# Attention's output set on feature rows through memory, divided there, and projected without transposes

## The chip, the cores and the metric

The kernel runs on one core of a Trainium2 chip. A core has five engines that run side by side, each through its own list of instructions in order: TensorE (PE in the profile; PEld is its weight load), VectorE (DVE), ScalarE (ACT), GpSimd (POOL) and SyncE (SP). SP does no arithmetic here; it issues nearly all transfers between HBM and the core's memory, in the order of its list, and a transfer that has to wait for something holds up all transfers behind it on SP. Matmul results land in PSUM, everything else lies in SBUF, both with 128 partitions.

The metric is the device time of one execution in microseconds (us). Lower is better.

## The reference

One sequence of 2048 rows with 256 features, all in float32. The program is

```python
x = x + attn_a(layernorm(x))   # 16 heads of 16, 4 key/value heads, rope, biases, causal
x = x + ffn(layernorm(x))      # 256 -> 2048 -> 256, 4-bit weights with scales, gelu gate
x = x + attn_b(layernorm(x))   # 16 heads of 16, no rope, causal
x = x + ffn(layernorm(x))      # the same weights again
```

and both attentions end in

```python
probs = jax.nn.softmax(scores, axis=-1)
attended = jnp.einsum('bhts,bshd->bthd', probs, v).reshape(B, S, hidden)
return attended @ Wo.T + bo
```

(the second has no bias). The change concerns what lies between the product with v and the product with Wo.

## The kernel before, in words

**Tiling.** The rows are cut into NB = 4 blocks of TB = 512, each of NT = 4 tiles of 128. The 16 heads are cut into NG = 4 groups of four. Attention works through 16 units (block b, group g), block by block. Because of the causal mask block b looks at 4(b + 1) key tiles, so a unit is short in block 0 (12 to 16 us where nothing else is done in it) and 41 to 54 us in block 3.

**A unit.** `value_steps(b, g)` gives the main list. `pair(kt, p)` makes the scores of two heads with key tile kt, keys on partitions and queries along the row (L716), subtracts the row maximum by a further matmul (L721), and lets ScalarE take the exponential (L729). `values(half)` multiplies the exponentials by v (L703), four heads at once, each into its own 32 partitions of one PSUM tile `ps_av`. Of the 32 partitions of a head the first 16 are its attended features, the 17th is the sum of the exponentials (v carries a column of ones), the others are padding. At the end of a unit `end()` copies this tile to SBUF as `o` (ScalarE, L739): features on partitions, queries along the row.

**Beside it** runs a side list. `weave` puts its steps between the main ones, in proportion. It has, above all, `max_steps` of the unit that follows: scores again, queries on partitions (L643), whose row maxima VectorE takes (L651), and a `gather` of them. Scores of both kinds use three PSUM buffers in turn (`ps_s`); a fourth, single tile (`ps_m`) serves everything else. In units g = 0 and 1 the side list also prepares the next block (`prep_steps`: layernorm, transposes, projections, bias and rope; the results go to HBM as a high and a low part and come back in another layout), and in the first attention a share of the dequantization of the MLP's weights. `load_q` for the unit after next stands at the head of each unit: eight transfers on SP, 64 KB each (L614).

**After a unit**, as the first step of the next one's side list, `divide()` transposes `o` in four pieces of 128x128 (L746), so that queries are on partitions; VectorE takes the reciprocals of the sums (L751) and multiplies (L754), into `self.att[b]`. When all four groups of a block are there, `out_steps` (in the next block's first unit) transposes att back in pieces, features on partitions (`turn`, L775), copies them as `aT` (ScalarE, L780), multiplies by Wo (`project`, L787) and adds to x (VectorE, L792). So each attended value is transposed twice: once to be divided, once to be projected.

**At the end of attention** the last `divide`, two empty steps and the last `out_steps` are handed to the MLP, as side steps among the features of its first block. A feature step is eight matmul records on TensorE (L876), then ScalarE, GpSimd and VectorE for the gelu gate. The side list there also prepares the MLP's second block. `Mlp.run` begins with the load of the down weights `wd`, 2 MB, on SP (L868).

Every engine runs its list in the order written[...].

Of the kernel before, what the change touches and what calls it, by code (L numbers as in the profile page):

```python
# [8 lines left out]
F32 = mybir.dt.float32  # L9
# [7 lines left out]
ALU = mybir.AluOpType  # L17
# [3 lines left out]
P = 128  # L21
S = 2048
D = 256
NH = 16
HD = 16
NKV = 4
NG = NH // 4
MLP = 2048
NFC = MLP // P
TB = 512  # L30
NB = S // TB
NT = TB // P
# [23 lines left out]
def blend(a, b):  # L56

    keyed = [((n + 0.5) / len(a), 0, n, f) for n, f in enumerate(a)]
    keyed += [((n + 0.5) / len(b), 1, n, f) for n, f in enumerate(b)]
    return [f for *_, f in sorted(keyed, key=lambda k: k[:3])]  # L60
# [3 lines left out]
def tile_hybrid_layers(  # L64
# [25 lines left out]
    nc = tc.nc  # L90
# [9 lines left out]
    small = ctx.enter_context(tc.tile_pool(name="small", bufs=2))  # L100
    pre = ctx.enter_context(tc.tile_pool(name="pre", bufs=1))
    psum = ctx.enter_context(tc.tile_pool(name="psum", bufs=1, space=PSUM))
    dram = ctx.enter_context(tc.tile_pool(name="dram", bufs=1, space=bass.MemoryType.DRAM))
# [7 lines left out]
    def ps_m():  # L111
        return psum.tile([P, 512], F32, tag="m", name="ps_m")
# [36 lines left out]
    for src, at in ((bq, 0), (bk, D), (bv, D + 64)):  # L149
        n = src.shape[1]  # L150
# [18 lines left out]
    ident = const.tile([P, P], F32, tag="ident", name="ident")  # L169
# [221 lines left out]
    class Attention:  # L391
# [293 lines left out]
        def value_steps(self, b, g):  # L685

            nk = NT * (b + 1)
            held = {"pending": []}

            def values(half):  # L690

                kt, q0, es_ = held["pending"][0]
                few = TB - q0 <= TB // 2
                if half == 1:
                    held["pending"].pop(0)
                    if few:
                        return
                elif kt == 0:
                    held["av"] = ps_av()
                own = slice(q0, TB) if few else slice(*((q0, TB // 2), (TB // 2, TB))[half])  # L700
                for j in range(4):
                    h = g if self.first else 4 * g + j
                    nc.tensor.matmul(  # L703
                        held["av"][32 * j : 32 * j + 32, own],
                        lhsT=self.vv[kt // NT][:, kt % NT, h * VW : h * VW + 32],
                        rhs=es_[j // 2][:, j % 2, own],
                        start=(kt == 0 and half == 0), stop=(kt == nk - 1),
                    )

            def pair(kt, p):  # L710
                q0 = max(0, kt - NT * b) * P
                diagonal = kt >= NT * b
                keys = slice((kt % NT) * P, (kt % NT + 1) * P)
                pt = ps_s()
                for r in range(2):
                    nc.tensor.matmul(  # L716
                        pt[:, r, q0:], lhsT=self.key_rows(kt // NT, g, p, r, keys),
                        rhs=self.qT[b, g][64 * r : 64 * r + 64, p, q0:], start=True, stop=False,
                    )
                for r in range(2):  # L720
                    nc.tensor.matmul(  # L721
                        pt[:, r, q0:], lhsT=sel[64 * r : 64 * r + 64, p, :],
                        rhs=self.mT[b, g][64 * r : 64 * r + 64, q0:],
                        start=False, stop=not diagonal,
                    )
                if diagonal:
                    self.add_mask(pt, 1, q0)
                e = self.wk.tile([P, 2, TB], F32, tag="e", name="e", bufs=4)
                nc.scalar.activation(e[:, :, q0:], pt[:, :, q0:], AF.Exp, scale=QK_SCALE)  # L729
                if p == 0:  # L730
                    held["es"] = [e]
                else:
                    held["pending"].append((kt, q0, held["es"] + [e]))

            def end():
                values(0)
                values(1)
                o = pre.tile([P, TB], F32, tag="o", name="o")
                nc.scalar.copy(o, held["av"])  # L739
                held["o"] = o  # L740

            def divide():
                o = held["o"]
                pt = ps_m()
                for i in range(NT):
                    nc.tensor.transpose(  # L746
                        pt[:, i * P : (i + 1) * P], o[:, i * P : (i + 1) * P], ident
                    )
                heads = pt.rearrange("p (t j c) -> p t j c", t=NT, c=32)
                rec = small.tile([P, NT, 4], F32, tag="rec", name="rec")  # L750
                nc.vector.reciprocal(rec, heads[:, :, :, HD])  # L751
                if g == 0:
                    self.att[b] = pre.tile([P, NT, NG, 4, HD], F32, tag="att", name="att")
                nc.vector.tensor_tensor(  # L754
                    self.att[b][:, :, g], heads[:, :, :, :HD],
                    rec.unsqueeze(3).broadcast_to([P, NT, 4, HD]), ALU.mult,
                )

            steps = []
            for kt in range(nk):  # L760
                for p in range(2):
                    steps.append(lambda kt=kt, p=p: pair(kt, p))
                    if kt:
                        steps.append(lambda p=p: values(p))
            return steps, end, divide

        def out_steps(self, b):
            held = {}

            def turn(n):  # L770
                pt = ps_m()
                for i in range(2):
                    flat = self.att[b][:, 2 * n + i].rearrange("p g j c -> p (g j c)")
                    for c in range(2):
                        nc.tensor.transpose(  # L775
                            pt[:, (2 * i + c) * P : (2 * i + c + 1) * P],
                            flat[:, c * P : (c + 1) * P], ident,
                        )
                aT = pre.tile([P, 2, 2, P], F32, tag="aT", name="aT")
                nc.scalar.copy(aT, pt.rearrange("p (i c t) -> p i c t", i=2, c=2))  # L780
                held[n] = aT

            def project(n):
                po = ps_m()
                for i in range(2):
                    for c in range(2):
                        nc.tensor.matmul(  # L787
                            po[:, i * D : (i + 1) * D], lhsT=held[n][:, i, c, :],
                            rhs=self.wo[:, c, :], start=(c == 0), stop=(c == 1),
                        )  # L790
                to = xt[b][:, 2 * n : 2 * n + 2, :]
                nc.vector.tensor_tensor(  # L792
                    to, po.rearrange("p (i d) -> p i d", i=2), to, ALU.add
                )

            return [lambda n=n, f=f: f(n) for n in range(2) for f in (turn, project)]

        def run(self, extra, beside):


            units = [(b, g) for b in range(NB) for g in range(NG)]
            per_unit = -(-len(extra) // (len(units) - NG))
            late, ahead = [], []
            for n, (b, g) in enumerate(units):
                more = []
                if g == 0 and b > 0:
                    more += self.out_steps(b - 1)
                if g == 0 and b + 1 < NB:
                    ahead = self.prep_steps(b + 1)
                    few = -(-len(ahead) // 2)  # L810
                if n >= NG:
                    more, extra = more + extra[:per_unit], extra[per_unit:]
                if g < 2:
                    more, ahead = more + ahead[:few], ahead[few:]
                if n + 2 < len(units):
                    self.load_q(*units[n + 2])
                steps, turn = [], None
                if n + 1 < len(units):
                    steps, turn = self.max_steps(*units[n + 1])
                else:  # L820
                    more += beside
                side = late + (blend(steps, more) if steps else more)
                steps, end, divide = self.value_steps(b, g)
                weave(steps, side, rest=4)
                if turn:
                    turn()
                end()
                late = [divide]
            return late + [lambda: None] * 2 + self.out_steps(NB - 1)


    class Mlp:
# [89 lines left out]
    at = Attention(True, wqkv_a)  # L922
    with tc.tile_pool(name="wk1", bufs=2) as wk, tc.tile_pool(name="kv1", bufs=1) as kv:
        at.wk = at.qpool = wk
        with tc.tile_pool(name="init", bufs=1) as pool:
# [13 lines left out]
            steps, turn = at.max_steps(0, 0)  # L939
# [5 lines left out]
    at = Attention(False, wqkv_b)  # L945
    with tc.tile_pool(name="kv20", bufs=1, reuse_waits="tile") as kv0, tc.tile_pool(
        name="wk2", bufs=2, reuse_waits="tile"
# [7 lines left out]
        steps, turn = at.max_steps(0, 0)  # L955
# [60 lines left out]
```

## Time and profile before

| | us |
|---|---|
| median of 3 runs (1912.67 to 1927.99) | 1915.32 |
| the profiled execution | 1916.85 |
| its span, first to last instruction | 1914.7 |
| TensorE busy | 1829.9 |
| VectorE busy | 1109.2 |
| ScalarE busy | 813.5 |
| GpSimd busy | 238.0 |

The profile is of one execution, so sums made from it are set against its own 1916.85 us. Attention of the first layer ends at 646.5 us, the first MLP runs to about 1007, the second attention ends at 1567.9, and the second MLP closes the span. "PE ... <- ACT aT L780" in a list of waits reads: TensorE stood still until ScalarE had written aT at line 780. The duration of a matmul includes the length of the pipeline; how much of TensorE one takes is the distance from its start to the start of the next. All engines but TensorE have idle time, which costs nothing in itself.

### The profile page before, as it was taken

The numbers are of one execution on the slowest core, as the hardware profiler recorded it, in microseconds if no ns is written. First come the engines' busy times: TensorE is split into PE (matmuls) and PEld (weight loads), VectorE is DVE, ScalarE is ACT, GpSimd is POOL, SyncE is SP. The second block draws the span as 40 slices with busy tenths as digits, with TensorE's granted clock in tenths as the row PEclk, the third lists the DMA queues.
The fourth block names the chain that finished last, engine by engine and source line by source line (L and its number), as shares of the span: only waits on it lengthen the run. The fifth ranks groups of instructions, "written<-read, shape, count | busy, mean of one in ns | idle before, by whom it ended". The sixth has DMA issues, their size and how long they took to land. (4 is left out here: it accounts for less than half of the span.)

```text
span 1914.7 us, 31770 instructions
## 1 busy us (share of the span) xinstructions
PE 1829.9 (96%) x13452; PEld 985.9 (51%) x13452; DVE 1109.2 (58%) x1612; ACT 813.5 (42%) x1069; POOL 238.0 (12%) x433
## 2 busy tenths in 40 slices
PE   5899989999999999999999999999999999999999
PEld 3454444444444456656565545445444444756656
DVE  4556677787776253444444667766867715363443
ACT  1334445465666521222214355556556662131221
POOL 3301311300001011112102010010000001011110
PEclk8879999999999999999999899999999999999999
DMA  4510320301101100002305050050000010000000
GB/s 102 131 45 23 72 46 23 73 23 23 34 23 34 45 6 0 1 0 47 75 1 111 24 100 23 13 100 23 13 13 1 2 46 0 11 1 11 6 6 11
DMA packets 42270, 64.23 MB, mean 34 GB/s; under 512 B 13840, under 2 KB 20880, under 8 KB 41872
## 3 DMA queue, kind: packets, MB, share of 16 engines
q1 hardware_dynamic: 33488, 45.93, 8.5%
q0 software_dynamic: 7680, 15.74, 5.1%
q8 instruction: 106, 1.74, 0.4%
q10 hardware_dynamic: 960, 0.52, 0.1%
q14 instruction: 36, 0.29, 0.1%
HBM read 44.24 MB, written 17.83 MB: 32 GB/s over the span
## 5 line engine op out<-in xcount | busy, mean ns | idle before, releaser
L729 ACT ACTIVATE e<-ps_s 128x1024 f32<-128x1024 f32 (+3 forms) x640 | 571.5, 897 | 457.8 <-PE ps_s L628 227.8
L651 DVE TENSOR_REDUCE mx<-ps_s 128x2 f32<-128x1024 f32 (+3 forms) x640 | 657.9, 1061 | 171.0 <-PE ps_s L643 85.9
L703 PE MATMUL ps_av<-e,v 128*32 128x256 f32 (+1 forms) x4608 | 363.9, 383 | 0.7 <-ACT e L729 0.7
L643 PE MATMUL ps_s<-kT,qT 64*128 64x512 f32 (+3 forms) x1280 | 281.8, 436 | 31.3 <-DVE mx L651 12.2
L716 PE MATMUL ps_s<-qT,kT 64*128 64x512 f32 (+3 forms) x1280 | 289.9, 449 | 11.4 <-DVE mx L651 6.1
L876 PE MATMUL ps_s<-xnT,wg 128*128 128x512 f32 x512 | 242.5, 596 | 0.0
L721 PE MATMUL ps_s<-mT,sel 64*128 64x512 f32 (+3 forms) x1280 | 240.9, 372 | 0.2 <-ACT mT L677 0.2
L876 PE MATMUL ps_s<-xnT,wu 128*128 128x512 f32 x512 | 240.6, 592 | 0.0
L643 PEld LDWEIGHTS ps_s<-kT,qT 64*128 64x128 f32 x1280 | 124.3, 187 | 186.1 <-issue 85.4
L716 PEld LDWEIGHTS ps_s<-qT,kT 64*128 64x128 f32 x1280 | 122.3, 187 | 158.6 <-issue 80.9
L884 DVE TENSOR_TENSOR t<-ps_s,t 128x512 f32<-128x512 f32 x128 | 88.2, 689 | 171.2 <-POOL t L883 169.4
L882 ACT ACTIVATE t<-ps_s 128x512 f32<-128x512 f32 x128 | 76.3, 596 | 249.9 <-PE ps_s L876 249.5
L885 ACT ACTIVATE t<-t 128x512 f32<-128x512 f32 x128 | 80.6, 630 | 201.2 <-DVE t L884 201.2
L703 PEld LDWEIGHTS ps_av<-e,v 128*32 128x32 f32 x4608 | 92.7, 108 | 136.6 <-issue 113.4
L876 PEld LDWEIGHTS ps_s<-xnT,wu 128*128 128x128 f32 x512 | 97.3, 190 | 122.5 <-issue 122.5
L883 POOL TENSOR_SCALAR t<-t 128x512 f32<-128x512 f32 x128 | 79.4, 620 | 577.7 <-ACT t L882 574.9
L876 PEld LDWEIGHTS ps_s<-xnT,wg 128*128 128x128 f32 x512 | 96.2, 192 | 106.4 <-issue 104.5
L886 DVE SCALAR_TENSOR_TENSOR t<-t,ps_s 128x512 f32<-128x512 f32 x128 | 88.1, 688 | 89.0 <-ACT t L885 89.0
L721 PEld LDWEIGHTS ps_s<-mT,sel 64*128 64x128 f32 x1280 | 124.5, 190 | 10.0 <-ACT mT L677 6.5
L628 PE MATMUL ps_s<-mask_t,mask_w 64*128 64x64 bf16 x2048 | 125.1, 199 | 0.0
L901 PE MATMUL ps_av<-wd,inter 128*128 128x256 f32 x512 | 114.5, 380 | 0.0
L901 PE MATMUL ps_m<-wd,inter 128*128 128x256 f32 x512 | 114.3, 380 | 0.0
(123 smaller groups left out, 1188.3 us busy)
## 6 DMA issues: line engine op xcount, KB each, us to landing
qT<-h SPq DMA_DIRECT2D x256, 64.0 KB, 2.3
kT<-h POOLq DMA_DIRECT2D x96, 128.0 KB, 6.1
h<-high SPq DMA_DIRECT2D x24, 256.0 KB, 3.0
h<-low SPq DMA_DIRECT2D x24, 256.0 KB, 3.3
wd<-wd_kept SPq DMA_DIRECT2D x2, 2048.0 KB, 7.8
wd_kept<-dq_d SPq DMA_DIRECT2D x4, 512.0 KB, 2.7
out<-x SPq DMA_DIRECT2D x16, 128.0 KB, 1.7
x<-x SPq DMA_DIRECT2D x3, 512.0 KB, 5.1
```

Of the source, the lines that this page charges most:

```text
L628: nc.tensor.matmul(pt[:, r, to], lhsT=mask_w[rows, kind, part, :], rhs=mask_t[rows, kind, part, :], start=False, stop=(part == 1),)
L643: nc.tensor.matmul(pt[:, r, :w], lhsT=self.qT[b, g][64 * r : 64 * r + 64, p, i * P : (i + 1) * P], rhs=self.key_rows(c, g, p, r, slice(0, w)),
L651: nc.vector.tensor_reduce(held["mx"][:, i, 2 * p : 2 * p + 2, c], pt[:, :, :w], AX.X, ALU.max)
L703: nc.tensor.matmul(held["av"][32 * j : 32 * j + 32, own], lhsT=self.vv[kt // NT][:, kt % NT, h * VW : h * VW + 32], rhs=es_[j // 2][:, j % ...
L716: nc.tensor.matmul(pt[:, r, q0:], lhsT=self.key_rows(kt // NT, g, p, r, keys), rhs=self.qT[b, g][64 * r : 64 * r + 64, p, q0:], start=True ...
L721: nc.tensor.matmul(pt[:, r, q0:], lhsT=sel[64 * r : 64 * r + 64, p, :], rhs=self.mT[b, g][64 * r : 64 * r + 64, q0:], start=False, stop=no ...
L729: nc.scalar.activation(e[:, :, q0:], pt[:, :, q0:], AF.Exp, scale=QK_SCALE)
L876: nc.tensor.matmul(pt[:, k, :], lhsT=w[:, c, fc * P : (fc + 1) * P], rhs=self.xnT[b][:, c, :], start=(c == 0), stop=(c == 1),)
L884: nc.vector.tensor_tensor(t, gate, t, ALU.mult)
L885: nc.scalar.activation(t, t, AF.Tanh, scale=GELU_C)
L886: nc.vector.scalar_tensor_tensor(t, t, 1.0, gate, ALU.add, ALU.mult)
L901: nc.tensor.matmul(po[:, :D], lhsT=inter[:, fc, i * P : (i + 1) * P], rhs=wd[:, fc, :], start=(fc == 0), stop=(fc == NFC - 1),)
```

## The change

`end()` no longer keeps `o` for a transpose. It writes it to HBM (`o_kept`, 256 KB) and at once reads two things back, all three transfers on SP: the 64 feature rows of the four heads, as dense rows, into one half of a tile `att` of 128 partitions, and the four rows of sums into `den`, cut into pieces of 32 so that they lie on 64 partitions. Two groups fill `att` and `den`; so `att[b, 0]` and `att[b, 1]` hold a block's 256 features on partitions, as the projection reads them.

After every odd group two steps go to the next unit: `invert` takes the reciprocals of `den` (VectorE), writes them to HBM and reads them back as `factor`, each head's row of 512 repeated on its 16 partitions (two transfers on SP, the second after the first has landed); `divide` multiplies att by it (VectorE). `turn` and `aT` are gone; `project` reads att as it is.

The places change too. `late` (invert, divide and, after a block's last group, the two projections) is put into the next unit's side list at positions 5, 12, 14 and 16, or at its end if it is shorter, in place of divide at its head and out_steps spread through it. At the end of attention the four steps go to the MLP without the two empty steps.

```diff
                 values(1)
                 o = pre.tile([P, TB], F32, tag="o", name="o")
                 nc.scalar.copy(o, held["av"])
-                held["o"] = o
+
+
+                kept = dram.tile([4, 32, TB], F32, tag="o", name="o_kept", bufs=2)
+                nc.sync.dma_start(out=kept.rearrange("j c t -> (j c) t"), in_=o)
+                if g % 2 == 0:
+                    self.att[b, g // 2] = (
+                        pre.tile([P, TB], F32, tag="att", name="att", bufs=2),
+                        small.tile([P, 32], F32, tag="den", name="den"),
+                    )
+                att, den = self.att[b, g // 2]
+                rows = slice(64 * (g % 2), 64 * (g % 2) + 64)
+                nc.sync.dma_start(
+                    out=den[rows], in_=kept[:, HD].rearrange("j (s q) -> j s q", q=32)
+                )
+                nc.sync.dma_start(out=att[rows], in_=kept[:, :HD])
+
+            def invert():
+                den = self.att[b, g // 2][1]
+                rec = small.tile([P, 32], F32, tag="rec", name="rec")
+                nc.vector.reciprocal(rec, den)
+
+                kept = dram.tile([8, TB], F32, tag="rec", name="rec_kept", bufs=2)
+                nc.sync.dma_start(
+                    out=kept.rearrange("h (s q) -> (h s) q", q=32), in_=rec
+                )
+                factor = pre.tile([P, TB], F32, tag="factor", name="factor")
+                nc.sync.dma_start(
+                    out=factor, in_=kept.unsqueeze(1).broadcast_to([8, HD, TB])
+                )
+                held["factor"] = factor
 
             def divide():
-                o = held["o"]
-                pt = ps_m()
-                for i in range(NT):
-                    nc.tensor.transpose(
-                        pt[:, i * P : (i + 1) * P], o[:, i * P : (i + 1) * P], ident
-                    )
-                heads = pt.rearrange("p (t j c) -> p t j c", t=NT, c=32)
-                rec = small.tile([P, NT, 4], F32, tag="rec", name="rec")
-                nc.vector.reciprocal(rec, heads[:, :, :, HD])
-                if g == 0:
-                    self.att[b] = pre.tile([P, NT, NG, 4, HD], F32, tag="att", name="att")
-                nc.vector.tensor_tensor(
-                    self.att[b][:, :, g], heads[:, :, :, :HD],
-                    rec.unsqueeze(3).broadcast_to([P, NT, 4, HD]), ALU.mult,
-                )
+                att = self.att[b, g // 2][0]
+                nc.vector.tensor_tensor(att, att, held["factor"], ALU.mult)
 
             steps = []
             for kt in range(nk):
...
                     steps.append(lambda kt=kt, p=p: pair(kt, p))
                     if kt:
                         steps.append(lambda p=p: values(p))
-            return steps, end, divide
+            return steps, end, [invert, divide] if g % 2 else []
 
         def out_steps(self, b):
-            held = {}
-
-            def turn(n):
-                pt = ps_m()
-                for i in range(2):
-                    flat = self.att[b][:, 2 * n + i].rearrange("p g j c -> p (g j c)")
-                    for c in range(2):
-                        nc.tensor.transpose(
-                            pt[:, (2 * i + c) * P : (2 * i + c + 1) * P],
-                            flat[:, c * P : (c + 1) * P], ident,
-                        )
-                aT = pre.tile([P, 2, 2, P], F32, tag="aT", name="aT")
-                nc.scalar.copy(aT, pt.rearrange("p (i c t) -> p i c t", i=2, c=2))
-                held[n] = aT
-
             def project(n):
                 po = ps_m()
                 for i in range(2):
+                    t = (2 * n + i) * P
                     for c in range(2):
                         nc.tensor.matmul(
-                            po[:, i * D : (i + 1) * D], lhsT=held[n][:, i, c, :],
+                            po[:, i * D : (i + 1) * D], lhsT=self.att[b, c][0][:, t : t + P],
                             rhs=self.wo[:, c, :], start=(c == 0), stop=(c == 1),
                         )
                 to = xt[b][:, 2 * n : 2 * n + 2, :]
...
                     to, po.rearrange("p (i d) -> p i d", i=2), to, ALU.add
                 )
 
-            return [lambda n=n, f=f: f(n) for n in range(2) for f in (turn, project)]
+            return [lambda n=n: project(n) for n in range(2)]
 
         def run(self, extra, beside):
 
...
             late, ahead = [], []
             for n, (b, g) in enumerate(units):
                 more = []
-                if g == 0 and b > 0:
-                    more += self.out_steps(b - 1)
                 if g == 0 and b + 1 < NB:
                     ahead = self.prep_steps(b + 1)
                     few = -(-len(ahead) // 2)
...
                     steps, turn = self.max_steps(*units[n + 1])
                 else:
                     more += beside
-                side = late + (blend(steps, more) if steps else more)
-                steps, end, divide = self.value_steps(b, g)
+                side = blend(steps, more) if steps else more
+
+                for at, step in zip((5, 12, 14, 16), late):
+                    side.insert(at, step)
+                steps, end, late = self.value_steps(b, g)
                 weave(steps, side, rest=4)
                 if turn:
                     turn()
                 end()
-                late = [divide]
-            return late + [lambda: None] * 2 + self.out_steps(NB - 1)
+                if g == NG - 1:
+                    late += self.out_steps(b)
+            return late
 
 
     class Mlp:
```

## The prediction

> **What bounds the kernel now.** First the page's head and busy times: which engine is full.
>
> ```profile
> span 1914.7 us, 31770 instructions
> PE 1829.9 (96%) x13452; PEld 985.9 (51%) x13452; DVE 1109.2 (58%) x1612; ACT 813.5 (42%) x1069; POOL 238.0 (12%) x433
> ```
>
> TensorE is busy 96% of the span, VectorE 58%. So work taken from TensorE is worth its own length wherever no other wait ends at the same moment, and a new wait on TensorE costs its whole length. Next the groups by form, for the matmul groups that the change deletes (count | busy us, mean ns of one | idle before):
>
> ```profile
> L746 PE MATMUL ps_m<-ident,o 128*128 128x128 f32 x128 | 22.2, 299 | 0.0
> L775 PE MATMUL ps_m<-ident,att 128*128 128x128 f32 x64 | 11.1, 300 | 2.7 <-DVE att L754 2.7
> ```
>
> These are all 192 transposes. The mean of 300 ns is the life of one pipelined instruction, not what it takes from TensorE; that is seen in the timeline, start to start, here in a unit with nothing late:
>
> ```profile
> 1335.52 0.49 PE L721 MATMUL ps_s<-mT,sel 64*128 64x512 f32 x2
> 1336.01 0.65 PE L746 MATMUL ps_m<-ident,o 128*128 128x128 f32 x4
> 1336.60 0.50 PE L716 MATMUL ps_s<-qT,kT 64*128 64x512 f32 x2
> ```
>
> Four transposes hold TensorE from 1336.01 to 1336.60: 0.59 us. Then the passage from attention to the first MLP (646.5 is the first feature of the MLP; the second passage, at 1567.9, looks the same):
>
> ```profile
> 646.52 1.98 PE L876 MATMUL ps_s<-xnT,wg 128*128 128x512 f32 x4
> 648.34 1.88 PE L876 MATMUL ps_s<-xnT,wu 128*128 128x512 f32 x4
> 650.06 0.60 PE L746 MATMUL ps_m<-ident,o 128*128 128x128 f32 x4
> 650.50 1.88 PE L876 MATMUL ps_s<-xnT,wg 128*128 128x512 f32 x4
> ...
> 661.24 1.89 PE L787 MATMUL ps_m<-wo,aT 128*128 128x256 f32 x8
> 662.96 1.88 PE L876 MATMUL ps_s<-xnT,wg 128*128 128x512 f32 x4
> ...
> 666.40 0.60 PE L775 MATMUL ps_m<-ident,att 128*128 128x128 f32 x4
> 669.81 3.00 PE L787 MATMUL ps_m<-wo,aT 128*128 128x256 f32 x8 [2.81 <-ACT aT L780]
> 672.61 2.60 PE L876 MATMUL ps_s<-xnT,wg 128*128 128x512 f32 x4
> 675.05 1.88 PE L876 MATMUL ps_s<-xnT,wu 128*128 128x512 f32 x4
> ```
>
> One feature takes 3.43 us of TensorE, four transposes 0.44 us here. The 2.81 us wait costs more than itself: L787, 1.72 us at 661.24, takes 2.80 us after it, and the next gate group 2.44 in place of 1.72. A gap of that size costs 1.8 us of slow matmuls on top.
>
> Last, what transfers take from issue to landing, and when the MLP's down weights go out (first and last start):
>
> ```profile
> qT<-h SPq DMA_DIRECT2D x256, 64.0 KB, 2.3
> h<-high SPq DMA_DIRECT2D x24, 256.0 KB, 3.0
> wd<-wd_kept SPq DMA_DIRECT2D x2, 2048.0 KB, 7.8
> mask_t<-mask_t SPq DMA_DIRECT2D x1, 32.0 KB, 2.4
> ```
> ```profile
> L868 SPq DMA_DIRECT2D wd<-wd_kept x2: 319/328/338, 646.1 to 1536.4; - x2
> ```
>
> **What goes.** (a) 192 transposes. In attention, 42 groups of four at 0.59 us: 24.8 us. In the two passages, 6 groups at 0.44: 2.6. Sum 27.4 us. Here the Trainium skill would promise more ("TensorE: Matmul & The Clock Gate", Part 4: PE-mode transpose): about 275 ns for one in a kernel. The trace has 272 to 273 as the usual duration too, but start to start only 147 or 110 ns. By the page 192 would be worth 52.8 us, by the timeline 27.4; I take the timeline, because the rest of that time already carries the next matmul.
>
> (b) Waits for the transposes' copies. In each passage L787 would have followed at 666.84 and came at 669.81: 2.97 us, and 1.80 of slow matmuls: 4.77, twice 9.5 us. In attention L775 waits 2.7 us for att (three times 0.90), and one projection 0.90 at 72.1: 3.6 us.
>
> (c) Off TensorE: 16 copies aT of 0.58 us on ScalarE (42% busy) and 32 reciprocals and products (0.26 + 0.43 us) on VectorE, against 16 reciprocals and 16 products of 128x512 now. For these I take 0.26 and 0.69 us (L792's size); a product with both operands in SBUF beside GpSimd could be 1.37, as the sum at L517 was. That is 15 to 26 us against 22: no change on an engine at 58%; if none of it were covered, 7 us less to 4 us more.
>
> Gain: 27.4 + 9.5 + 3.6 = 40.5 us.
>
> **What comes: a chain through memory.** From the start of the copy o: copy 0.6; write o_kept, 256 KB as h<-high, 3.0: at 3.6; den from there 2.3: at 5.9. SP issues den and att (to 4.5), then the eight qT loads that stood ahead and now stand behind them, at 0.49 each (seven took 3.42 at 218.6): to 8.4. The loads are late by some 4 us, but their first reader is a unit later, 12.4 us at the shortest: no cost; with no cover it would be those 4 us. The writes of the next block's queries and keys (high, low) and the dequantization loads stand behind the chain on SP too, but come later in the unit than 13.7 us or are read a unit later: nothing. After the even groups the chain stops at att, which nobody reads until the odd group is done: nothing. The write of rec cannot be issued before 8.4, nor before VectorE has run the reciprocal: 2.3 us for 16 KB in 128-byte rows (between the 2.3 of qT and the 2.4 of mask_t), at 10.7; factor, 256 KB, 3.0: at 13.7. The product waits until 13.7 with all further row maxima queued behind it on VectorE, and for those TensorE's score buffers wait.
>
> When would VectorE come to it? I counted the row maxima (L651) that precede each new instruction in the changed order and looked up when the same one ends in this trace, less the deleted TensorE work ahead of it. The reciprocal is reached at 4.7 to 9.6 us: at most 1.2 early, covered. The product, for the seven odd groups of each layer that are followed by another attention unit: first layer 12.8, 9.3, 11.2, 8.3, 14.0, 14.5, 14.4; second 9.9, 10.7, 15.4, 10.9, 15.7, 16.9, 16.8. Two of these (12.8 and 9.9, after block 0's second group) have it last in their list: the next maximum starts at 17.7 and 14.4, so nothing waits. Five are early, by 4.4, 2.5, 5.4, 3.0 and 2.8 us. TensorE goes on meanwhile through one score and one pair with its values, until the three score buffers are taken, about 1.5 us (two steps); or until the projection, two side steps later. Cost: 2.9 + 1.0 + 3.9 + 1.5 + 1.3 = 10.6 us. Bounds: 4 (cover of 3 us) to 22 (no cover, slow matmuls after two).
>
> The passages are worse. The padding before out_steps is gone: reciprocal and product both follow feature 0, the first projection feature 1, the second feature 2. Counted from feature 0's first matmul: den is there at 6.0; feature 0's last VectorE operation ends 7.9 (654.4 in this trace); reciprocal 8.1. The write of rec goes to SP behind wd. That transfer went out at 646.1 and 1536.4; now it is behind o_kept, den and att in both layers, is issued at about 4.8 and lands at 12.6. No row shows a small write behind 2 MB. On its own it lands at 10.5. The Trainium skill ("DMA: Bandwidth & Descriptors", Queues, rings and completion order) says that each DMA engine consumes a queue's descriptors in ring order, so it would land with wd, 12.6. I take 12.6, because both are on SP's queue; then factor 15.6, product 16.3. TensorE finishes feature 1 at 6.9 and stands at the projection for 9.4 us, then 1.8 of slow matmuls: 11.2, twice 22.4. Landing at 10.5 it would be 9.1 each, 18.2. Ends: 15 (no slow matmuls, no queueing) and 28.
>
> The 64 projection matmuls are unchanged: att's feature rows are the stationary operand where aT was.
>
> **Sum.** -40.5 + 10.6 + 22.4 = -7.5 us. The profiled execution took 1916.85 (span 1914.7 and 2.15 around it), so 1909.3; the median of the runs is 1.5 lower: 1908.
>
> **Rivals.** *The chain is mostly hidden.* TensorE keeps working 3 us into each stall (attention 3.8), rec lands before wd (18.2) and half of the slow restarts do not happen: -40.5 + 3.8 + 16.4 = -20.3: 1895. For it: three score buffers, VectorE at 58%. Against it: in the passage the projection stands in order on TensorE, and no buffer helps there.
>
> *The round trip decides: slower.* If factor lands later than 13.7, more units wait, since seven of the twelve that matter are reached between 14.0 and 16.9. At 15 the attention cost is 17 and the passages add 3: 1917, the end of the gain. At 17: 32 and 29, 1936. At 19: about 56 and 33: 1964. It needs 3.3 us more over four transfers, with rows of 128 bytes in two of them, nothing like which is in this trace. I give it 1937.
>
> *VectorE keeps the pace.* In the units before each new block VectorE is busy 17 to 40 us of 21 to 43, and TensorE waits for row maxima. If a third of the 24.8 us in attention is lost to that, 1916. Against it: VectorE loses 0.69 us in just these units.
>
> **Chances.** My sum 0.50, hidden 0.20, round trip 0.18, VectorE 0.12. About 1% (1896 to 1934) is what a measurement can tell from no change: faster 0.16, same 0.67, slower 0.17. The range reaches from the hidden chain with better cover (1890) towards the round-trip case, 1931.
>
> **What would show it.** No L746 or L775 group on TensorE. A wait of TensorE for the product att of 8 to 11 us at the first projection of each passage; wd issued some 5 us into it, rec's landing with or before wd's. VectorE idle before att for a DMA of factor, a few us in five units, none after block 0's second group. Factor landing 13 to 14 us after the start of o's copy. I am wrong if small rows take far over 2.3 us, or if the projection waits under 5 us in the passages.

## The result, and the profile after

The changed kernel takes 1974.44 us (median of 4 runs, 1974.09 to 1979.55), against 1921.38 us for the kernel before in the same comparison: ratio 1.028, 95% interval 1.025 to 1.031. It is slower. The prediction was 1908, range 1890 to 1931: a little faster, and it came out slower and outside the range.

The profiled execution has a span of 1977.8 us, 63.1 more than before; it is the slowest of the four (1979.55 us, the others 1974.1 to 1974.5). The head of the page, its busy row for TensorE and the row of the granted TensorE clock (40 equal slices, tenths of full speed), after:

```profile
span 1977.8 us, 31607 instructions
PE 1831.6 (93%) x13260; PEld 980.3 (50%) x13260; DVE 1105.0 (56%) x1580; ACT 804.0 (41%) x1053; POOL 237.8 (12%) x433
PEclk8788889899999989999999899999999998999999
```

192 matmuls fewer, and TensorE's busy time has not fallen (1829.9 before): many of the others ran slower, as the clock row shows against that of before:

```profile
PEclk8879999999999999999999899999999999999999
```

The groups by form have no transposes of `o` or `att` any more; in their place stand the projection and the product, both with long idle time ahead:

```profile
L789 PE MATMUL ps_m<-wo,att 128*128 128x256 f32 x128 | 42.3, 477 | 33.6 <-DVE att L773 33.6
L773 DVE TENSOR_TENSOR att<-att,factor 128x512 f32<-128x512 f32 x16 | 11.0, 689 | 43.8 <-DMA factor<-rec_kept 43.8
```

To see where the time went, both traces are cut at the starts of the copies of `o`. Units are counted from 0 (unit = 4b + g; the second attention is 16 to 31), and the stretch of a unit ends where its own copy starts. A passage is the stretch from the last copy of an attention over the whole MLP. The differences, after less before:

| stretches | us |
|---|---|
| 0 (before any changed instruction, so not from the change) | +4.5 |
| 4, 5, 6, 8, 9 (first attention, blocks 1 and 2) | +8.4, +11.2, +8.4, +4.5, +8.4 |
| 1 and 17 (second unit of block 0, both attentions) | +3.4, +5.4 |
| the two passages to the MLP | +6.9, +6.4 |
| 10, 19, 20, 24 | +2.1, +1.6, +1.3, +3.5 |
| all others together | -12.9 |

The passage was foreseen. The timeline of TensorE there, after (start and length in us, engine, line, operation; in brackets the idle time just before and what ended it):

```profile
697.35 1.88 PE L880 MATMUL ps_s<-xnT,wu 128*128 128x512 f32 x4
699.06 0.59 PE L789 MATMUL ps_m<-wo,att 128*128 128x256 f32 x2
709.75 2.93 PE L789 MATMUL ps_m<-wo,att 128*128 128x256 f32 x6 [10.10 <-DVE att L773]
712.48 3.57 PE L880 MATMUL ps_s<-xnT,wg 128*128 128x512 f32 x4
715.88 1.88 PE L880 MATMUL ps_s<-xnT,wu 128*128 128x512 f32 x4
```

and SP's own timeline beside it:

```profile
692.82 0.32 SPq L743 DMA_DIRECT2D o_kept<-o  x1
694.83 0.54 SPq L751 DMA_DIRECT2D den<-o_kept  x1
695.41 0.53 SPq L754 DMA_DIRECT2D att<-o_kept  x1
696.31 0.32 SPq L872 DMA_DIRECT2D wd<-wd_kept  x1
700.30 0.33 SPq L762 DMA_DIRECT2D rec_kept<-rec  x1
705.29 0.60 SPq L766 DMA_DIRECT2D factor<-rec_kept  x1
```

`factor` goes out when `rec` has landed: 5.0 us after `rec` here, behind the 2 MB of `wd`, against 1.42 us in stretch 14, where nothing is ahead of it.

The largest part was not foreseen. The list of waits (us in total, times, longest), before:

```profile
DVE dq_t L339 <- POOL dq_b L328: 1.3, 1, 1.3
PE ps_s L716 <- DVE mx L651: 6.1, 17, 0.8
```

and after:

```profile
DVE dq_t L339 <- POOL dq_b L328: 50.8, 7, 10.9
DVE att L773 <- DMA factor<-rec_kept: 43.8, 11, 8.7
PEld ps_m L789 <- DVE att L773: 36.4, 6, 10.5
PE ps_s L716 <- DVE mx L651: 24.8, 17, 6.6
```

VectorE waits 50.8 us for `dq_b`, the packed weights that GpSimd has unpacked from a load on SP. The head of stretch 5 shows why. SP before (o is copied at 180.0), then SP after (o at 194.9):

```profile
178.79 3.57 SPq L614 DMA_DIRECT2D qT<-h  x8
182.46 0.37 SPq L314 DMA_DIRECT2D dq_q<-up_p  x1
```
```profile
195.48 0.32 SPq L743 DMA_DIRECT2D o_kept<-o  x1
197.49 0.53 SPq L751 DMA_DIRECT2D den<-o_kept  x1
198.11 0.52 SPq L754 DMA_DIRECT2D att<-o_kept  x1
198.72 5.38 SPq L614 DMA_DIRECT2D qT<-h  x8
204.21 0.51 SPq L314 DMA_DIRECT2D dq_q<-up_p  x1
```

Before, SP was ahead of the other engines and the load went out 2.5 us after the copy; now it goes out at 9.3. VectorE takes the unpacked weights at the same place in its list as before, right behind two row maxima. VectorE before, then after:

```profile
183.73 1.23 DVE L651 TENSOR_REDUCE mx<-ps_s 128x2 f32<-128x1024 f32 x1 [0.19 <-PE ps_s L643]
186.24 0.23 DVE L339 TENSOR_SCALAR dq_t<-dq_b 128x128 uint32<-128x128 uint32 x1 [1.28 <-POOL dq_b L328]
```
```profile
197.78 1.23 DVE L651 TENSOR_REDUCE mx<-ps_s 128x2 f32<-128x1024 f32 x1 [0.59 <-PE ps_s L643]
208.03 0.23 DVE L339 TENSOR_SCALAR dq_t<-dq_b 128x128 uint32<-128x128 uint32 x1 [9.02 <-POOL dq_b L328]
```

All further row maxima stand behind that wait, and TensorE's score buffers behind those. The windows of this stretch (length, busy time of TensorE, its weight loads, VectorE, ScalarE, GpSimd; then the clock), before and after:

```profile
180.00:219.50 39.50, 36.10 (x318) 17.72 (x318) 25.86 (x41) 16.42 (x23) 15.54 (x24) 1.00 0.41 87
```
```profile
194.90:245.50 50.60, 41.75 (x314) 19.80 (x313) 25.25 (x39) 16.36 (x23) 15.50 (x24) 0.86 0.34 76
```

TensorE's idle time in it grew by 5.5 us, the stretch by 11.2; the rest is slow matmuls: the clock fell from 1.00 to 0.86.

The writes of the next block's queries and keys come late in the same way. In stretch 17 (o is copied at 1024.7 before, at 1077.1 after) the first `high` goes out 6.7 us after the copy before, 13.1 after. SP before, then after, and what TensorE then waits for:

```profile
1023.88 3.66 SPq L614 DMA_DIRECT2D qT<-h  x8
1031.33 0.34 SPq L535 DMA_DIRECT2D h<-high  x1
```
```profile
1082.76 7.34 SPq L614 DMA_DIRECT2D qT<-h  x8
1090.19 0.37 SPq L535 DMA_DIRECT2D h<-high  x1
```
```profile
1095.90 3.78 PE L548 MATMUL ps_m<-wqkv_b,xnT 128*128 128x256 f32 x8 [3.86 <-DVE low L536]
```

### The profile page after: what moved, and what is told of

The parts are those of the page before. It is cut to its first block, busy times and chain, and to the rows that moved or that the text cites. A ratio compares the mean times of both kernels' runs of the same rounds, so it can differ in the third digit from the quotient of the medians.

```text
span 1977.8 us, 31607 instructions
## 1 busy us (share of the span) xinstructions
PE 1831.6 (93%) x13260; PEld 980.3 (50%) x13260; DVE 1105.0 (56%) x1580; ACT 804.0 (41%) x1053; POOL 237.8 (12%) x433
## 5 line engine op out<-in xcount | busy, mean ns | idle before, releaser
L716 PE MATMUL ps_s<-qT,kT 64*128 64x512 f32 (+3 forms) x1280 | 298.6, 457 | 32.8 <-DVE mx L651 24.8
L643 PE MATMUL ps_s<-kT,qT 64*128 64x512 f32 (+3 forms) x1280 | 290.0, 445 | 37.2 <-ACT e L729 17.2
L721 PE MATMUL ps_s<-mT,sel 64*128 64x512 f32 (+3 forms) x1280 | 246.8, 376 | 0.2 <-ACT mT L677 0.2
L643 PEld LDWEIGHTS ps_s<-kT,qT 64*128 64x128 f32 x1280 | 130.8, 192 | 193.4 <-issue 95.9
L721 PEld LDWEIGHTS ps_s<-mT,sel 64*128 64x128 f32 x1280 | 129.7, 193 | 9.2 <-ACT mT L677 6.7
```

The source lines that it names most:

```text
L643: nc.tensor.matmul(pt[:, r, :w], lhsT=self.qT[b, g][64 * r : 64 * r + 64, p, i * P : (i + 1) * P], rhs=self.key_rows(c, g, p, r, slice(0, w)),
L716: nc.tensor.matmul(pt[:, r, q0:], lhsT=self.key_rows(kt // NT, g, p, r, keys), rhs=self.qT[b, g][64 * r : 64 * r + 64, p, q0:], start=True ...
L721: nc.tensor.matmul(pt[:, r, q0:], lhsT=sel[64 * r : 64 * r + 64, p, :], rhs=self.mT[b, g][64 * r : 64 * r + 64, q0:], start=False, stop=no ...
```

## The experiments

Three theories were set against each other. A: SP's queue is the cause; what stands behind the chain there comes late. B: the late `factor` is the cause, wherever it is waited for. C: the passages. (Where an expectation below has letters of its own, it says what they stand for there.) Each experiment has as baseline the kernel before, run on the same chip (1917 to 1920 us).

**The packed weights on another queue.** In the changed kernel, one word in `load`, in both of its branches (the line is shortened):

```diff
-                nc.sync.dma_start(out=q, in_=src) if ... else nc.sync.dma_start(
+                nc.scalar.dma_start(out=q, in_=src) if ... else nc.scalar.dma_start(
```

> The changed kernel with the twelve loads of the packed weights (dq_q) issued by ScalarE in place of SP; nothing else differs. Theory A (on SP these loads stand behind o_kept, den, att and the eight qT loads, GpSimd then unpacks late, and VectorE waits 4 to 11 us in front of the row maxima in six units of the first attention): VectorE's waits for dq_b fall from 50.8 us to under 8 us, the granted clock between units 4 and 9 returns towards 1.00, and the time falls from 1974 to between 1938 and 1950. Theory B (the late factor is what costs, in every unit and both attentions): the waits for factor stay and the time falls by less than 8 us, to 1966 or more.

Measured 1956.03 us, ratio to before 1.018 (1.014 to 1.023). VectorE's wait for `dq_b` fell to 7.5 us; stretches 4, 5 and 9 got 6.9, 12.3 and 9.2 us shorter. But 6 and 8 hardly changed. The head of stretch 6 of this kernel on SP and VectorE:

```profile
245.32 0.37 SPq L762 DMA_DIRECT2D rec_kept<-rec  x1
249.05 0.60 SPq L766 DMA_DIRECT2D factor<-rec_kept  x1
```
```profile
253.00 0.69 DVE L773 TENSOR_TENSOR att<-att,factor 128x512 f32<-128x512 f32 x1 [8.29 <-issue]
```

There VectorE now stands 8.3 us before the product instead. The view names no releaser; the product starts 3.95 us after the issue of `factor`, and where it waits for `factor` in the change it starts 3.5 to 4.9 us after that issue. The gain, 18 us, is below A's range and well above B's: the loads are a cause, and where a factor is due in the same unit its wait lay underneath. A part of the shortfall in the trace stays open: stretches 2 and 3 are 4.2 and 4.3 us longer than in the change, at a granted clock of 0.50 and 0.57 and with no new wait of TensorE, and 22 is 5.3 longer, with VectorE waiting 4.5 us for its factor.

**Padding in the passage.**

```diff
-            return late
+            idle = [lambda: None]
+            return late[:1] + idle * 8 + late[1:2] + idle + late[2:3] + idle + late[3:]
```

> The changed kernel with eight empty steps between invert and divide and one each before the two projections when attention hands over to the MLP, so that the product comes after feature 6 and the projections after features 7 and 8. Theory A (in the passage TensorE stands at the projection for the factor, 10.1 and 9.8 us, and then runs slow for some 2 us): both waits vanish, each passage gets 11 to 13 us shorter, the time falls from 1974 to 1948 to 1952. Theory B (the passage loses to the load of wd or to the order of the MLP's own preparation): less than 10 us in all.

Measured 1965.46, ratio 1.022 (1.018 to 1.027): 9 us less than the change, where 22 to 26 were expected. In its trace the passages are 5.2 and 6.0 us shorter. The wait at the projection is down to 0.95 us, but the MLP's own preparation, pushed into the last features, now waits for its copies (TensorE's timeline):

```profile
712.94 1.56 PE L789 MATMUL ps_m<-wo,att 128*128 128x256 f32 x6 [0.95 <-DVE att L773]
...
747.92 0.70 PE L857 MATMUL ps_m<-ident,xn 128*128 128x128 f32 x2 [2.52 <-ACT xnT L858]
```

**The first half of the chain alone, in the kernel before.**

```diff
                 held["o"] = o
+                kept = dram.tile([4, 32, TB], F32, tag="o", name="o_kept", bufs=2)
+                nc.sync.dma_start(out=kept.rearrange("j c t -> (j c) t"), in_=o)
...
+                nc.sync.dma_start(out=den[rows], in_=...)
+                nc.sync.dma_start(out=att[rows], in_=kept[:, :HD])
```

> The kernel before, complete, with three transfers added after each unit on SP: o written to HBM, and den and att read back from there into tiles that nobody uses. Transposes, order of steps and padding are as before. Theory A (SP's queue alone carries most of the loss, through the dequantization loads and the high and low writes behind the chain): 30 to 45 us slower than before, in units 1, 4, 5, 6, 8 and 9 of the first attention, with VectorE waiting for dq_b, and within 5 us in the second attention. Theory B (factor is the cost; SP's waits are hidden): within 8 us of before.

Measured 1945.45, ratio 1.013 (1.009 to 1.018), 26 us slower than 1919.76: a little under A's range, far outside B's. In the trace +10.0 in stretch 5, +3.0 in 6, +2.6 in 8, +8.5 in 9, and +2.7 and +3.7 in 1 and 17; in the rest of the second attention nothing. Stretch 4 did not grow, against A. VectorE's waits:

```profile
DVE dq_t L339 <- POOL dq_b L328: 21.7, 4, 7.3
```

**The same with the packed weights on ScalarE's queue, and a control.**

> The kernel before with the twelve loads of the packed weights issued by ScalarE in place of SP; nothing else. Control for the other two: if moving the loads gains nothing where nothing stands ahead of them, within 3 us of before.

> The kernel before with the unused chain o_kept, den, att added on SP (1945 against 1920 without it) and the packed weights' loads on ScalarE's queue. If the loads standing behind the chain are the cause, units 5, 6, 8 and 9 return to within 2 us each of before, and 4 to 8 us remain, in units 1 and 17, where the high and low writes of the next block stand behind the chain: 1923 to 1929. If the transfers as such slow those units, it stays at 1940 or more.

The control took 1919.81, ratio 1.0005 (0.9986 to 1.0024), within the 3 us expected: moving the loads gains nothing by itself. With the chain 1925.38, ratio 1.002 (1.000 to 1.005), as expected: of the chain's 26 us 20 are gone. What is left in the trace stands in stretches 1 and 17, +3.2 each, where the `high` and `low` writes stand behind the chain; no run moves these writes alone. 5 and 6 are as long as in the control to 0.3 us. So 32 times three transfers cost next to nothing as transfers. What costs is what queues behind them.

**Without the second half.** This kernel leaves out `invert` and `divide`: the attended values stay undivided, and it serves for timing alone.

```diff
-            return steps, end, [invert, divide] if g % 2 else []
+            return steps, end, [lambda: None] * 2 if g % 2 else []
```

> The changed kernel without invert and divide: no reciprocal, no rec, no factor, no product, so the attended values stay undivided; o_kept, den, att and the projections are as in the change. This leaves the first half of the chain alone. If the first half carries the loss through SP's queue, the units 4 to 9 of the first attention stay 20 to 25 us slower than before, the passages lose nothing, and the time is 1925 to 1940. If the factor is the main cause, the time is below before, at 1890 to 1905, by the transposes and their waits.

Measured 1920.38, ratio 0.9996 (0.998 to 1.002). Stretches 4 to 9 stay 27 us longer than before together (4 itself only 1.2), `dq_b` is waited for 49.1 us, and the passages are 5 to 6 us shorter than before. The time lies between the two ranges. With the first half alone the change has lost all its gain; the second half takes another 54 us. By the trace the passages have 24 of these, which leaves, as an estimate, some 30 for the factor in attention. Neither A nor B is the whole.

**Later places.**

```diff
-                for at, step in zip((5, 12, 14, 16), late):
+                for at, step in zip((5, 20, 23, 25), late):
```

> The changed kernel with the late steps at positions 5, 20, 23 and 25 of the side list in place of 5, 12, 14 and 16. If the wait for the factor is a loss of its own in attention (about 28 us of VectorE's waits in nine units, 12 us of TensorE's at the projection), most of these waits go and the time falls by 10 to 18 us, to 1956 to 1964. If those units are slow only because SP's queue is late, the waits move to the dequantization and the time falls by less than 5.

Measured 1953.22, ratio 1.016 (1.013 to 1.020), 21 us less than the change: more than expected. VectorE's wait for `factor` fell from 43.8 to 23.6 us, of which 18.4 are the passages; the wait for `dq_b` stayed (46.8).

**The three edits together.**

> Three edits together on the changed kernel: the packed weights loaded by ScalarE's queue (1974 to 1956 alone), the padding in the passages (to 1965 alone) and the later places 5, 20, 23, 25. If the three causes are separate, the gains add up, 18 + 9 + 12: 1935. If they cover each other (a wait removed shows the next one in the same unit), less. If moving the divide also frees what the loads alone left (units 6 and 8, where the factor took the place of the unpacking), more: 1920 to 1930.

Measured 1899.02, ratio 0.988 (0.985 to 0.992): 75 us less than the change, where the three alone give 18 + 9 + 21 = 48, and below the 1920 to 1930 expected at best. They covered each other: in stretches 6 and 8 the wait for the weights lay over the wait for the factor, and taking one left the other. Stretch 6 is 24.8 us here (33.3 in the change, 34.2 and 30.7 with one edit).

**The chain behind the loads.** No queue is changed; only order and places (shortened: a line in brackets stands for several):

```diff
+PLACES = (4, 7, 12, 22, 25, 27)   # keep, fetch, invert, divide, project, project
...
-                (o_kept, den, att at the end of the unit)
+            def keep():               # o_kept
+            def fetch():              # den, att
...
-            return steps, end, [invert, divide] if g % 2 else []
+            return steps, end, [keep, fetch] + ([invert, divide] if g % 2 else [])
```

> The changed kernel with the chain moved within SP's queue and in time, nothing added: o_kept is written by a step of the next unit, behind the qT loads and the packed weights' load (position 4), den and att are read at 7, invert stands at 12, divide at 22, the projections at 25 and 27, each going over into the unit after when a list is shorter; at the passages invert comes after feature 0 and divide and projections eight, ten and twelve steps into the MLP's own list. If SP's order and the places are all that is wrong with the change, what is left is its gain (0.5 us in each of 32 units, some 4 us of waits in attention and 5 us in each passage): 1893 to 1903, faster than before. If the transfers themselves cost (traffic, slow landing), it stays above before's 1915 to 1920.

Measured 1891.85, ratio 0.985 (0.981 to 0.988): faster than before, and just under the 1893 to 1903 expected. SP at the head of stretch 5 (o is copied at 177.1), and the two projections of the first passage:

```profile
175.84 3.59 SPq L615 DMA_DIRECT2D qT<-h  x8
179.53 0.37 SPq L315 DMA_DIRECT2D dq_q<-up_p  x1
180.00 0.38 SPq L745 DMA_DIRECT2D o_kept<-o  x1
183.56 0.54 SPq L759 DMA_DIRECT2D den<-o_kept  x1
184.15 0.52 SPq L762 DMA_DIRECT2D att<-o_kept  x1
```
```profile
676.98 1.89 PE L797 MATMUL ps_m<-wo,att 128*128 128x256 f32 x8
685.57 1.89 PE L797 MATMUL ps_m<-wo,att 128*128 128x256 f32 x8
```

The load is where it was before, the projections wait for nothing, and no product waits for its factor. The passages are 6.5 and 6.6 us shorter than before. The same transfers run as in the change.

> chain_behind_loads (1892) with the packed weights' loads on ScalarE's queue as well. VectorE still waited 2.4 to 4.4 us for the unpacked weights in three units there, and units 5, 6 and 9 were 1.5 us longer each than before: 2 to 6 us faster than 1892, if those waits come from SP; the same within 2 us, if not.

This took 1888.84, ratio 0.984 (0.981 to 0.987). The two stood in different comparisons, with almost the same interval, so a difference of 3 us between them is not shown.

**What a transpose is worth.** In the kernel before, `divide` with `for i in (*range(NT), *range(NT))`:

> The kernel before with the four transposes of each divide done twice into the same PSUM tile: 128 transposes more on TensorE, nothing else. If a transpose takes 0.147 us of TensorE in attention (0.59 us for four, start to start), the time grows by 17 to 20 us; if the pipeline hides part of it, by less than 10; if it takes the 0.27 us of its record, by 35.

Measured 1926.42 against 1919.76, ratio 1.0026 (1.0012 to 1.0040), so 2 to 8 us for 128 transposes: not the 17 to 20 of 0.147 us each, but the case in which the pipeline hides part of it. In the trace nearly every unit is 0.43 us longer, 0.108 for a transpose, which would be 13.8 in all. A second four right behind a first four is cheaper than the 0.59 us of the first, but why the timed runs show still less stays open.

## Why the prediction was wrong, point by point

**What goes (40.5 us): right in kind, somewhat large.** In units with no other difference (13 to 15 and 29 to 31) the change saves 0.3 to 0.8 us, 0.53 in the mean, where 0.59 was put. The waits of the passages went when the steps were placed well (6.5 and 6.6 us shorter; 4.8 + 1.3 had been put). With order and places mended, the change is 25 to 30 us faster than before by the medians: 63 to 75% of the 40.5. The doubled transposes gave less than their share, so the split between transposes and waits is less certain than the sum. The 1.37 us feared for a product is no instruction's: it is the mean of the two full-size sums at L517, 0.69 and 2.05 us. All 16 products took 0.68 to 0.69.

**"The writes ... and the dequantization loads stand behind the chain on SP too, but come later in the unit than 13.7 us or are read a unit later: nothing."** This is the step that failed. It put these transfers at nothing without a look at when they go out. In the trace of before, ten of the twelve loads are issued 1.5 to 3.7 us after the copy of `o`, not later than 13.7, and the reader on VectorE stands a few row maxima later in the same unit. It had been early because SP, waiting for nothing, ran ahead of the other engines; the change made SP wait for ScalarE's copy, for the landing of `o_kept` (61.2 us in all on SP) and, in the eight qT loads, for the landing of `att` (45.1). In the change these ten went out 8.7 to 11.4 us after the copy. Shown: by the weights on another queue (-18), by the unused chain in the kernel before (+26) and by the weights' queue there (-20). The writes fail the same way in stretches 1 and 17, +3.2 to +5.4 us each: before, their first `high` goes out 7.0 and 6.7 us after the copy. That is read from the traces, not from a run of its own.

**The factor in attention: 10.6 us put, bounds 4 to 22.** Too small. Later places alone gave 21 us, and more in company; some 30 are the estimate from the kernel without the second half. Two terms were mis-sized. The product's time: 13.7 us after the copy was put; in the second attention, where nothing else is late, it came at 14.8 and 14.9 (units 20 and 24), because the qT loads took 5.4 us of SP rather than 3.9 and `factor` 3.6 to 3.8 rather than 3.0 (`rec` took 1.8, less than the 2.3 put). In the first attention, where SP was late already and in unit 4 the reciprocal too stood behind the wait for `dq_b`, it came at 21.3 and 19.1 (units 4 and 6). And the price of a wait: 1.5 us of it was held to be covered, with full clock after. The clock fell instead in stretches 4, 5, 6, 8 and 9, to 0.86 in 5 and 0.80 in 6 (1.00 before in both).

**The passages: right.** A wait of 9.4 us was put at the projection, 10.1 and 9.8 came; a net loss of 5.1 us each (11.2 less the 4.8 and 1.3 saved), 6.9 and 6.4 came. The choice between the two ends was right as well: `rec` took 5.0 and 4.8 us behind `wd`. That agrees with the Trainium skill ("DMA: Bandwidth & Descriptors", Queues, rings and completion order), by which each DMA engine takes a queue's descriptors in ring order; it was the better guide than the row of a small write alone. No run issues `rec` from another queue, so how much of it is the queue and how much the traffic of 2 MB stays open.

**The sum of the terms.** As an estimate from these runs: 25 to 30 us of gain, against 27 in stretches 4 to 9 from the first half, some 30 from the factor in attention and 24 in the passages, makes 51 to 56 us slower; 53 were measured. The prediction had 0, 10.6 and 22.4 for the three losses.

**The rivals.** "The round trip decides" had the right sign, and some of its mechanism is there: `factor` late in attention. But it looked at VectorE's waits for the chain's own result. A third to a half of the loss (18 us by moving the loads, 26 by the chain alone, of 53) comes from work that has nothing to do with it and only shares the queue. VectorE's pace, the fourth case, was not seen as a loss: of the six units before a new block, 3, 7, 11, 23 and 27 are 0.5 to 1.7 us shorter, and 19 is 1.6 longer.

## What to carry to other kernels

A transfer whose issue waits for something closes its queue: before putting one in, list what stands behind it there and how early each reader needs it, also where the reader belongs to other work. Put the transfers that wait behind those that don't, and give each round trip its measured time before the first in-order engine asks for it; here that alone turned 2.8% slower into 1.5% faster. Where two waits fall into the same unit, taking one away shows little until the other goes too.

## What the runs showed of the hardware

Short stops of TensorE were followed by a halved clock. In stretch 5 of the change TensorE stood from 205.4 to 209.1 us, and from 210.7 to 220.9 its granted clock was 0.50. Its idle time grew by 5.5 us in that stretch, and the stretch by 11.2. In 6, 8 and 9 idle time grew by 5.2, 3.6 and 5.9, the stretches by 8.4, 4.5 and 8.4: 1.3 to 2 times the stop. In 4, where the clock was 0.89 before already, 9.0 us of idle time made 8.4. No run holds the clock still to part the two exactly. The Trainium skill ("TensorE: Matmul & The Clock Gate", Why this matters for your kernels) asks for no idle gap above some 3 us between bursts; the gaps in stretches 4 to 9 that late row maxima caused are of 3.8 to 6.6 us. In the passage of before the 2.81 us gap was already enough: the granted clock was 0.50 from 670.7 to 674.0.

Moving twelve loads to a second queue changed nothing where the first queue was free (1919.81 against 1919.12) and gave 20 us where it was held up (1945.45 to 1925.38).
